# A Flamingo gated layer on one core: the output projection by a 26-product scheme in place of seven products

## The chip, the cores and the metric

The kernel runs on one core of one Trainium2 chip. The metric is the device time of one execution in microseconds (us), here the median of three runs. A profile is one execution recorded by the hardware profiler, with a duration of its own. PE is TensorE's matmul, PEld its weight load, DVE VectorE, ACT ScalarE, POOL GpSimd, SP SyncE (it issues most DMAs).

## The reference

All arrays are fp32. x and ctx are 64 x 128 x 512 (sequences, tokens, DIM). The parts that matter:

```python
xn = layernorm(x)
Q, K, V = heads(xn) @ Wh, heads(ctx) @ Wh, heads(ctx) @ Wh       # 4 heads of 128
A = maximum(abs((Q K^T / sqrt(128) * decay).sum(over the batch)), 1)
Y = groupnorm_like(A @ V) * gamma + beta                         # over DIM
W = relu(xn @ wg)                                                # 512 x 512
x = x + tanh(g_xattn) * ((W * Y) @ wo)                           # wo: 512 x 512
h = silu(ln(x) @ gate_w.T * gate_s) * (ln(x) @ up_w.T * up_s)    # 512 -> 1408
x = x + tanh(g_ffn) * ((h @ down_w.T) * down_s)                  # 1408 -> 512
```

The change is in `(W * Y) @ wo` and its weights alone.

## The kernel before

**Groups.** The 64 sequences are worked on in 16 groups of four (512 tokens, four token tiles of 128). Pass 1 (to about 400 us) normalises every group, sums the scores over the batch, and prepares the weights: `prepare_weights` loads each weight, scales it, forms the sums that the fast schemes need, and writes weights and sums to scratch in DRAM (stores at L481). For wo that is `load_wo` and `sum_wo`: one DVE scale, four POOL sums (L324), seven stores of 256 KB to `wo_scr`.

**Pass 2.** For every group g, `attended(g)` does the output projection, the residual add into the tiles x_t, and the second layer norm; `ffn(g)` does the gated feed-forward part. Ahead of that, `next_retention(g)` makes the gate products W (L287, with adds at L578 and L581 in group 0's neighbourhood), A @ V (`po`, L652/L654), the normalised Y, and W * Y, in the tiles w_t (L711). The generators are interleaved at their yields: in regular groups `ffn(g)` runs beside `attended(g+1)` and then `next_retention(g+2)`. Group 0's projection has only the end of pass 1's work beside it: `in_order("ATATATAAAAAPAPAPAPA", A=attended(0, ...), T=tail, P=...)`. The yields set the order of the text; a list scheduler in the framework then fixes each engine's order of instructions before the launch, and `tc.issue_after` adds constraints to it. Each engine then runs its own list in that order, and waits at semaphores.

**The output projection before.** The 512 x 512 by 512 x 512 product of one group is a 2 x 2 block product by a scheme of seven half-size products. `combine_a` forms four sums (`ys`, 128x512 each) of the four input blocks on `helper`, which is VectorE for groups 0 to 2 and POOL later (L327 to L330). `wo_product` (L725 to L737) loads one weight tile of 256 KB (`wo_w`, L727, tag "wo", three buffers, on SP) and issues four matmuls of 128x128 by 128x256 (L730) into a PSUM bank: bx, bz, bx, by, bz, by, by. After each product the whole bank, 128x512, is added into x_t on DVE (L741); the first is copied by ACT to m1 (L751) and added three times by POOL (L741). A yield stands after each product, and x_t's tiles come from DRAM by `load_x` (L186, pool of five).

**The feed-forward part.** Gate and up use the same seven-product scheme (`product`, L287, banks a, b, c, f), with DVE at L965, L880 and L912 to L918 and ACT at L879; the block that seven products leave over is at L890 to L918 ("rest"), its weights `gu_rest`. The gate/up weights are the tiles `gu` (L849, SP). The down projection already uses the 26-product scheme: `DOWN_STEPS` is a list of 24 steps; a step names an accumulator (c1, a, f, b0, c0, b1), the products that it adds up (indices of a sum of the input, and of a sum of the weights) and the blocks of the output that receive it, with their signs. `H_SUMS` are 28 sums or differences of 128x128 input blocks (L335, `sum_tiles`), `W_SUMS` 18 of 128x256 weight blocks. The down products are L1006, their adds into x_t L1026 (128x256). `last_down` is the last down product issued; the next projection's first product is held behind it.

**PSUM.** Of the eight banks of 128x512 fp32, five belong to the feed-forward part and three (`ps_mm`, tag "mm") rotate among the projection's bx, by, bz and others.

Of the kernel before, what the change touches and what calls it, by code (L numbers as in the profile page):

```python
# [10 lines left out]
F32 = mybir.dt.float32  # L11
AF = mybir.ActivationFunctionType
ALU = mybir.AluOpType
# [10 lines left out]


GA11, GS1, GA12, GS2, GS3, GS4, GA22 = range(7)
DB11, DB21, DB22, DT1, DT2, DT3, DT4 = range(7)

# [7 lines left out]
DOWN_SIGN = (-1, -1, 1, 1, -1, 1, 1, 1)  # L36
H_SLOTS, H_SLOTS3, H_EARLY = 26, 20, 8
H_SUMS = (
# [6 lines left out]
)  # L45
# [6 lines left out]
W_SUMS = (  # L52
# [4 lines left out]
)  # L57
# [13 lines left out]
DOWN_STEPS = (  # L71
    ("c1", ((2, 2, 1),), ((5, -1),)),
    ("a", ((0, 0, 13),), ((0, -1),)),
    ("f", ((8, 8, 10),), ((1, 1),)),
    ("b0", ((20, 1, 12),), ((4, 1), (6, -1),)),
    ("c0", ((6, 6, 2),), ((4, 1),)),
    ("c1", ((22, 13, 15),), ((7, 1),)),
    ("a", ((1, 16, 23),), ((1, -1),)),
    ("f", ((25, 19, 19),), ((0, 1),)),
# [47 lines left out]
def flamingo_gated_layer(  # L127
# [21 lines left out]
    nc = tc.nc  # L149
    P = 128  # L150
    B, S, DIM = x.shape
    H = wh.shape[0]
    INTER = gateT.shape[1]
    NC = DIM // P
    NI = INTER // P
    GB = 4
    NG = B // GB
    TOK = GB * S
    HT = TOK // 2
    HN = DIM // 2  # L160
    KC = NC // 2
# [7 lines left out]
    dram = ctx.enter_context(tc.tile_pool(name="dram", bufs=1, space=DRAM))  # L169
    xin = ctx.enter_context(tc.tile_pool(name="xin", bufs=5))  # L170
    att = ctx.enter_context(tc.tile_pool(name="att", bufs=1))
    wide = ctx.enter_context(tc.tile_pool(name="wide", bufs=2))
    stat = ctx.enter_context(tc.tile_pool(name="stat", bufs=4))
    ps_mm = ctx.enter_context(tc.tile_pool(name="ps_mm", bufs=3, space=PSUM))
    ps_bank = ctx.enter_context(tc.tile_pool(name="ps_bank", bufs=1, space=PSUM))

    last_load, last_norm, last_down, mid_down = [None], [None], [None], [None]
# [40 lines left out]

    gu_scr = [dram.tile([NJ, P, n, 2, KC, P], F32, name=f"gu_scr{n}") for n in (3, 4)]
    dn_scr = dram.tile([26, P, 3, HN], F32, name="dn_scr")  # L220
    wo_scr = dram.tile([7, P, KC, HN], F32, name="wo_scr")
    sq_scr = [
        [dram.tile([P, NQ, NC, GB * SQ], F32, name=f"sq_scr{n}{i}") for i in range(2)]
        for n in range(2)
# [11 lines left out]
    for seeded in (bank_b, bank_c0, bank_c1):  # L236
        for i in range(TOK // P):
            nc.tensor.matmul(
                seeded[:, i * P : (i + 1) * P], lhsT=ident, rhs=ident,
                start=(i == 0), stop=True, skip_group_check=True,  # L240
# [79 lines left out]
    def combine_b(engine, t, b11, b12, b21, b22):  # L320
        for dst, in0, in1 in (
            (t[0], b12, b11), (t[1], b22, t[0]), (t[2], b22, b12), (t[3], b21, t[1]),
        ):
            engine.tensor_tensor(dst, in0, in1, ALU.subtract)  # L324

    def combine_a(engine, s, a11, a12, a21, a22):
        engine.tensor_tensor(s[0], a21, a22, ALU.add)  # L327
        engine.tensor_tensor(s[1], s[0], a11, ALU.subtract)
        engine.tensor_tensor(s[2], a11, a21, ALU.subtract)
        engine.tensor_tensor(s[3], a12, s[1], ALU.subtract)  # L330

    def sum_tiles(engine, slots, sums):

        for to, a, b, sign in sums:
            engine.tensor_tensor(  # L335
                slots[to], slots[a], slots[b], ALU.add if sign == "+" else ALU.subtract
            )
# [4 lines left out]
    once = pass1.enter_context(tc.tile_pool(name="once", bufs=1))  # L342
# [4 lines left out]
    for m, k, e in ((GA11, 0, 0), (GA12, 1, 0), (7, 0, 1), (GA22, 1, 1)):  # L347
        for s in range(2):
            e0 = e * HN + s * P
            nc.sync.dma_start(  # L350
                out=wgc[:, m, s],
                in_=wg[k * HN : (k + 1) * HN, e0 : e0 + P].rearrange("(k p) i -> p k i", p=P),
# [9 lines left out]
    tanh_g = const.tile([P, 2], F32, name="tanh_g")  # L362
# [5 lines left out]
    for h in range(H):  # L368
        nc.tensor.matmul(
            pg[:, h, :], lhsT=whT_sb[:, h, :], rhs=whT_sb[:, h, :],  # L370
            start=True, stop=True,
# [29 lines left out]
    RAW = [P, 8, 2, KC, P]  # L401

    def load_wo():
        raw = once.tile([P, NC, DIM], F32, tag="raw", name="wo_raw", bufs=2)
        nc.sync.dma_start(out=raw, in_=wo.rearrange("(c p) e -> p c e", p=P))
        return raw

    def sum_wo(raw):

        nc.vector.tensor_scalar_mul(ds, ds, tanh_g[:, 1:2])  # L410
        nc.vector.tensor_scalar_mul(raw, raw, tanh_g[:, 0:1])
        t = once.tile([P, 4, KC, HN], F32, tag="sums", name="wo_t")
        b = (
            raw[:, 0:KC, 0:HN], raw[:, 0:KC, HN:DIM], raw[:, KC:NC, 0:HN], raw[:, KC:NC, HN:DIM],
        )
        combine_b(nc.gpsimd, [t[:, i] for i in range(4)], *b)
        return [
            (wo_scr[m], src)
            for m, src in zip(range(7), (b[0], b[2], b[3], t[:, 0], t[:, 1], t[:, 2], t[:, 3]))
        ]  # L420

    def load_down(n):
        raw = once.tile([P, 16, HN], F32, tag="raw", name="dn_raw", bufs=2)
# [168 lines left out]
    for g in range(NG):  # L592
        x_t, c_t = x_next.pop(0), c_next
# [122 lines left out]
    def attended(g, x_t, ws, x1nT):  # L716

        helper = nc.vector if g < 3 else nc.gpsimd

        a11, a21, a12, a22 = ws[0][:, 0], ws[1][:, 0], ws[0][:, 1], ws[1][:, 1]  # L720
        s = att.tile([P, 4, KC, HT], F32, tag="sq", name="ys")
        combine_a(helper, [s[:, i] for i in range(4)], a11, a12, a21, a22)
        yield

        def wo_product(bank, m, lhs, start):  # L725
            w = att.tile([P, KC, HN], F32, tag="wo", name="wo_w", bufs=3)
            nc.sync.dma_start(out=w, in_=wo_scr[m])  # L727
            for i in range(2):
                for k in range(KC):
                    nc.tensor.matmul(  # L730
                        bank[:, i * HN : (i + 1) * HN],
                        lhsT=lhs[:, k, i * P : (i + 1) * P],
                        rhs=w[:, k, :],
                        start=(start and i == 0 and k == 0),
                        stop=(i == 1 and k == KC - 1),
                        skip_group_check=True,
                    )  # L737

        def add(engine, q, cols, src):
            dst = x_t[q][:, :, cols]  # L740
            engine.tensor_tensor(dst, dst, src.rearrange("p (b d) -> p b d", b=2), ALU.add)  # L741

        d1, d2 = slice(0, HN), slice(HN, DIM)
        bx = ps_mm.tile([P, TOK], F32, tag="mm", name="bx")
        if last_down[0] is None:
            wo_product(bx, DB11, a11, True)
        else:
            with tc.issue_after(last_down[0].ins):
                wo_product(bx, DB11, a11, True)
        m1 = att.tile([P, TOK], F32, tag="m1", name="m1")  # L750
        nc.scalar.copy(m1, bx)  # L751
        for q, d in ((0, d2), (1, d2), (1, d1)):
            add(nc.gpsimd, q, d, m1)
        yield
        bz = ps_mm.tile([P, TOK], F32, tag="mm", name="bz")
        wo_product(bz, DT1, s[:, 0], True)
        add(nc.vector, 1, d2, bz)
        yield
        wo_product(bx, DB21, a12, False)
        add(nc.vector, 0, d1, bx)  # L760
        yield
        by = ps_mm.tile([P, TOK], F32, tag="mm", name="by")
        wo_product(by, DT2, s[:, 1], True)
        add(nc.vector, 0, d2, by)
        yield
        wo_product(bz, DB22, s[:, 3], False)
        add(nc.vector, 0, d2, bz)
        yield
        wo_product(by, DT3, s[:, 2], False)
        add(nc.vector, 1, d2, by)  # L770
        yield
        wo_product(by, DT4, a22, False)
        add(nc.vector, 1, d1, by)
        yield

        if g:
            sq = att.tile([P, NQ, NC, GB, SQ], F32, tag="sq", name="sq")
        for j in range(GB):
            xb = x_t[j // 2][:, j % 2, :]
            mv = stat.tile([P, 2], F32, tag="mv", name="mv")  # L780
            bn(mv, xb)
            rs = stat.tile([P, 1], F32, tag="rs", name="rs")
            inv_std(rs, mv[:, 1:2], LN_EPS, 1)
            x1n = normalised(xb, mv[:, 0:1], rs)
            if g:
                square_transposed(sq, j, x1n)
            else:
                pt = transposed(x1n, "pt")
                nc.scalar.copy(
                    x1nT[:, :, :, j, :].rearrange("p i c b -> p c i b"),  # L790
                    pt.rearrange("p c (i b) -> p c i b", i=NQ),
                )
            yield
        if g:
            moved(x1nT, sq, sq_scr[1][g % 2])
# [8 lines left out]
    ws = None  # L804
# [10 lines left out]
    x_t = x_next.pop(0)  # L815
# [242 lines left out]
    for g in range(NG - 1):  # L1058
        x_t = x_next.pop(0)
# [75 lines left out]
```

## Time and profile before

| | |
|---|---|
| median of three runs | 2254.69 us (2254.12 to 2256.78) |
| profiled execution | 2253.64 us, of which the span is 2251.8 us |
| granted clock, mean | 0.998 |
| DMA traffic | 558.46 MB, 248 GB/s |
| wo_w loads | 112 of 256 KB, median 3.6 us from issue to landing |
| period of a regular group | 114.13 us (starts of the first bank_a product: 1193.83, 1307.96, 1422.08) |

The span runs from the first to the last instruction; the rest of the profiled execution's time, 1.84 us, lies around it. Times in views are us from the span's start. Busy TensorE time is a sum of modelled durations; the distance between starts of consecutive matmuls is the surer measure of what one costs.

### The profile page before, as it was taken

The numbers are of one execution on the slowest core, as the hardware profiler recorded it, in microseconds if no ns is written. First come the engines' busy times: TensorE is split into PE (matmuls) and PEld (weight loads), VectorE is DVE, ScalarE is ACT, GpSimd is POOL, SyncE is SP. The second block draws the span as 40 slices with busy tenths as digits, with TensorE's granted clock in tenths as the row PEclk, the third lists the DMA queues.
The fourth block names the chain that finished last, engine by engine and source line by source line (L and its number), as shares of the span: only waits on it lengthen the run. The fifth ranks groups of instructions, "written<-read, shape, count | busy, mean of one in ns | idle before, by whom it ended". The sixth has DMA issues, their size and how long they took to land.

```text
span 2251.8 us, 28752 instructions
## 1 busy us (share of the span) xinstructions
PE 2218.9 (99%) x10112; PEld 1889.7 (84%) x10112; DVE 1190.2 (53%) x2863; ACT 603.3 (27%) x1132; POOL 654.0 (29%) x1038
## 2 busy tenths in 40 slices
PE   8999999999999999999999999999999999999999
PEld 7878787778888888888888888888888888888888
DVE  6456543646454646464646464646464646454524
ACT  3444445322222222222222222222221212121221
POOL 4125300240323333333333333323232324141220
PEclk9999999999999999999999999999999999999999
DMA  9788855678777777777777777777777777766654
GB/s 300 263 279 308 287 190 176 253 240 260 255 269 240 265 249 256 258 248 266 247 267 236 257 247 266 239 262 243 268 237 269 236 272 233 280 205 243 223 184 145
DMA packets 216863, 558.46 MB, mean 248 GB/s; under 512 B 21264, under 2 KB 62992, under 8 KB 199952
## 3 DMA queue, kind: packets, MB, share of 16 engines
q1 hardware_dynamic: 211296, 539.58, 70.9%
q10 hardware_dynamic: 5424, 17.04, 2.0%
q8 instruction: 81, 1.33, 0.2%
q14 instruction: 62, 0.51, 0.1%
HBM read 454.31 MB, written 102.24 MB: 247 GB/s over the span
## 4 chain that ended last, share of the span: by engine, by line
PE 84%; DVE 6%; DMA 5%; POOL 3%; issue 1%; SPq 1%; ACT 0%; ACTq 0%; DVEq 0%; POOLq 0%
PE bank_c L287 18%; PE bank_a L287 12%; PE bank_c L1006 9%; PE bank_b L1006 6%; PE bank_f L287 6%; PE bank_b L287 6%; PE bank_f L1006 4%; PE bank_a L1006 4%; PE by L730 3%; PE sv L538 3%; PE bx L730 3%; PE bz L730 2%; PE po L652 2%; DMA gu_scr<-gu_raw 2%; DVE st L251 2%; PE bank_c L890 2%
## 5 line engine op out<-in xcount | busy, mean ns | idle before, releaser
L287 PE MATMUL bank_c<-tcomb,gu 128*128 128x256 f32 x1920 | 454.9, 380 | 0.7 <-DVE c L965 0.7
L287 PEld LDWEIGHTS bank_c<-tcomb,gu 128*128 128x128 f32 x1920 | 363.3, 190 | 59.3 <-issue 6.7
L335 POOL TENSOR_TENSOR h<-h 128x128 f32<-128x128 f32 x576 | 253.2, 470 | 398.5 <-DVE h L880 282.1
L287 PE MATMUL bank_a<-x1nT,gu 128*128 128x256 f32 x1280 | 305.5, 381 | 11.2 <-DVE h L880 9.6
L287 PEld LDWEIGHTS bank_a<-x1nT,gu 128*128 128x128 f32 x1280 | 241.8, 190 | 62.2 <-DVE h L880 14.8
L1006 PE MATMUL bank_c<-dn_w,h 128*128 128x256 f32 x896 | 211.7, 379 | 0.0
L1006 PEld LDWEIGHTS bank_c<-dn_w,h 128*128 128x128 f32 x896 | 170.2, 190 | 23.2
L879 ACT ACTIVATE sil<-c,gs_sb 128x256 f32<-128x256 f32 x176 | 89.3, 508 | 336.4 <-DVE c L965 171.7
L965 DVE TENSOR_TENSOR c<-bank_c,m 128x512 f32<-128x512 f32 x80 | 55.3, 691 | 219.5 <-PE bank_c L287 219.5
L247 POOL TENSOR_TENSOR rs<-ve,mhalf 128x1 f32<-128x1 f32 x128 | 73.4, 585 | 322.7 <-DVE ve L246 209.8
L711 POOL TENSOR_TENSOR w_t<-w_t,yT 128x256 f32<-128x256 f32 x112 | 91.6, 847 | 258.0 <-ACT yT L702 258.0
L741 POOL TENSOR_TENSOR x_t<-x_t,m 128x512 f32<-128x512 f32 x48 | 62.1, 1323 | 341.4 <-ACT m L751 341.4
L1006 PE MATMUL bank_b<-dn_w,h 128*128 128x256 f32 x640 | 156.4, 379 | 0.0
L335 DVE TENSOR_TENSOR h<-h 128x128 f32<-128x128 f32 x608 | 152.8, 312 | 4.3
L287 PE MATMUL bank_f<-tcomb,gu 128*128 128x256 f32 x640 | 151.2, 379 | 0.0
L287 PE MATMUL bank_b<-x1nT,gu 128*128 128x256 f32 x640 | 151.2, 379 | 0.0
L287 PEld LDWEIGHTS bank_b<-x1nT,gu 128*128 128x128 f32 x640 | 121.6, 190 | 22.1 <-issue 6.2
L287 PEld LDWEIGHTS bank_f<-tcomb,gu 128*128 128x128 f32 x640 | 121.6, 190 | 17.0 <-issue 0.5
L1006 PEld LDWEIGHTS bank_b<-dn_w,h 128*128 128x128 f32 x640 | 121.6, 190 | 16.5
L251 DVE BATCH_NORM_STATS2 st<-x_t 128x6 f32<-128x512 f32 x128 | 83.7, 682 | 79.3 <-DMA x_t<-in_x_dram 78.2
L538 PE MATMUL sv<-qw,c_t 128*128 128x256 f32 x512 | 122.0, 383 | 3.3 <-DVE xnT L513 3.3
L1026 DVE TENSOR_TENSOR x_t<-x_t,bank_c 128x256 f32<-128x256 f32 x192 | 77.8, 420 | 86.9 <-PE bank_c L1006 86.8
(150 smaller groups left out, 3260.8 us busy)
## 6 DMA issues: line engine op xcount, KB each, us to landing
dn_w<-dn_scr SPq DMA_DIRECT2D x320, 384.0 KB, 4.9
gu<-gu_scr SPq DMA_DIRECT2D x80, 1024.0 KB, 7.8
gu<-gu_scr SPq DMA_DIRECT2D x80, 768.0 KB, 5.9
x_t<-in_x_dram SPq DMA_DIRECT2D x62, 512.0 KB, 5.3
sq_scr<-sq SPq DMA_DIRECT2D x30, 1024.0 KB, 4.8
wo_w<-wo_scr SPq DMA_DIRECT2D x112, 256.0 KB, 3.6
dn_w<-dn_scr SPq DMA_DIRECT2D x96, 256.0 KB, 5.2
c_t<-in_ctxT_dram SPq DMA_DIRECT2D x64, 256.0 KB, 4.9
```

The lines of the kernel that those rows point to most:

```text
L247: nc.gpsimd.tensor_tensor(dst, ve, mhalf[:, :n], ALU.pow)
L251: nc.vector.bn_stats(st, src)
L287: nc.tensor.matmul(out, lhsT=w[:, s, k, :], rhs=x_k, start=(start and s == 0 and k == 0), stop=(s == 1 and k == KC - 1), skip_group_check= ...
L335: engine.tensor_tensor(slots[to], slots[a], slots[b], ALU.add if sign == "+" else ALU.subtract)
L538: nc.tensor.matmul(sv[:, 0 : 2 + i : 1 + i, :], lhsT=c_t[j][:, h, :], rhs=qw[:, h, j : GB + 1 : GB - j, :], start=(i == 0), stop=(i == 1), ...
L711: (helper if d else nc.gpsimd).tensor_tensor(w, w, yT[:, :, d * KC + k, q * 2 : q * 2 + 2, :], ALU.mult)
L730: nc.tensor.matmul(bank[:, i * HN : (i + 1) * HN], lhsT=lhs[:, k, i * P : (i + 1) * P], rhs=w[:, k, :], start=(start and i == 0 and k == 0 ...
L741: engine.tensor_tensor(dst, dst, src.rearrange("p (b d) -> p b d", b=2), ALU.add)
L879: nc.scalar.activation(sil, gate, AF.Silu, scale=gs_sb[:, i : i + 1])
L965: nc.vector.tensor_add(c22, bank_c, m5)
L1006: last_down[0] = nc.tensor.matmul(places[acc], lhsT=hq[q][:, a, :], rhs=dn[n][:, q, :], start=start, stop=True, skip_group_check=True,)
L1026: add = nc.vector.tensor_tensor(dst, dst, places[acc], ALU.add if sign > 0 else ALU.subtract)
```

## The change

The output projection takes over the 26-product scheme of the down projection: four token tiles, four tiles of DIM as the inner dimension, and two halves of the output. A group now has 26 single matmuls of 128x128 by 128x256, in the order of `DOWN_STEPS` (first indices). The 28 `H_SUMS` are formed on `helper`, partly in place in the w_t tiles, partly in ten tiles `more` (tag "sq", name ys). The six accumulators lie in halves of the three banks: c1 and b0 in bx, a and c0 in by, f and b1 in bz. After each step one to two DVE adds or subtractions of 128x256 go into x_t, 28 in all; ACT's copy m1 and POOL's adds are gone. A weight tile of 256 KB serves two products: 13 loads, three buffers as before. A yield stands after every fourth product. In the preparation `sum_wo` scales eight blocks by 128x256 with their signs on DVE, forms 18 sums on POOL and makes 26 stores of 128 KB. In the changed kernel the matmul is L751, the weight load L745, the x_t add L762, the down products L995 and their adds L1015.

```diff
-    wo_scr = dram.tile([7, P, KC, HN], F32, name="wo_scr")
+    wo_scr = dram.tile([13, P, 2, HN], F32, name="wo_scr")
...
     def load_wo():
-        raw = once.tile([P, NC, DIM], F32, tag="raw", name="wo_raw", bufs=2)
-        nc.sync.dma_start(out=raw, in_=wo.rearrange("(c p) e -> p c e", p=P))
+        raw = once.tile([P, 16, HN], F32, tag="raw", name="wo_raw", bufs=2)
+        nc.sync.dma_start(
+            out=raw[:, 0 : 2 * NC].rearrange("p (c d) e -> p c d e", d=2),
+            in_=wo.rearrange("(c p) (d e) -> p c d e", p=P, d=2),
+        )
         return raw
...
-        nc.vector.tensor_scalar_mul(raw, raw, tanh_g[:, 0:1])
-        t = once.tile([P, 4, KC, HN], F32, tag="sums", name="wo_t")
...
-        combine_b(nc.gpsimd, [t[:, i] for i in range(4)], *b)
...
+        for i, sign in enumerate(DOWN_SIGN):
+            nc.vector.tensor_scalar(
+                raw[:, i], raw[:, i], tanh_g[:, 0:1], float(sign), ALU.mult, ALU.mult
+            )
+        more = once.tile([P, 10, HN], F32, tag="sums", name="wo_t")
+        slots = [raw[:, i] for i in range(16)] + [more[:, i] for i in range(10)]
+        sum_tiles(nc.gpsimd, slots, W_SUMS)
+        order = [w for _, products, _ in DOWN_STEPS for _, _, w in products]
+        return [(wo_scr[n // 2, :, n % 2], slots[w]) for n, w in enumerate(order)]
...
-        a11, a21, a12, a22 = ws[0][:, 0], ws[1][:, 0], ws[0][:, 1], ws[1][:, 1]
-        s = att.tile([P, 4, KC, HT], F32, tag="sq", name="ys")
-        combine_a(helper, [s[:, i] for i in range(4)], a11, a12, a21, a22)
+        more = att.tile([P, H_SLOTS - 16, P], F32, tag="sq", name="ys")
+        slots = [
+            ws[b // 2][:, k // KC, k % KC, b % 2 * P : (b % 2 + 1) * P]
+            for k in range(NC) for b in range(GB)
+        ]
+        slots += [more[:, i] for i in range(H_SLOTS - 16)]
+        sum_tiles(helper, slots, H_SUMS)
         yield
-        def wo_product(bank, m, lhs, start):
...
-        def add(engine, q, cols, src):
...
+        banks = [ps_mm.tile([P, TOK], F32, tag="mm", name=name) for name in ("bx", "by", "bz")]
+        left, right = slice(0, HN), slice(HN, TOK)
+        places = {
+            "c1": (0, left), "a": (1, left), "f": (2, left),
+            "b0": (0, right), "c0": (1, right), "b1": (2, right),
+        }
+        begun = [None, None, None]
+        after = last_down[0]
+        n = 0
+        for acc, products, to in DOWN_STEPS:
+            bank, cols = places[acc]
+            sums = banks[bank][:, cols]
+            for a, _, _ in products:
+                if n % 2 == 0:
+                    w = att.tile([P, 2, HN], F32, tag="wo", name="wo_w", bufs=3)
+                    nc.sync.dma_start(out=w, in_=wo_scr[n // 2])
+                with ExitStack() as order:
+                    if after is not None:
+                        order.enter_context(tc.issue_after(after.ins))
+                    if begun[bank] is not None:
+                        order.enter_context(tc.issue_after(begun[bank].ins))
+                    first = nc.tensor.matmul(
+                        sums, lhsT=slots[a], rhs=w[:, n % 2],
+                        start=begun[bank] is None, stop=True, skip_group_check=True,
+                    )
+                begun[bank] = begun[bank] or first
+                n += 1
+                if n % 4 == 0:
+                    yield
+            for block, sign in to:
+                b, d = block // 2, block % 2
+                dst = x_t[b // 2][:, b % 2, d * HN : (d + 1) * HN]
+                nc.vector.tensor_tensor(dst, dst, sums, ALU.add if sign > 0 else ALU.subtract)
         yield
```

More of the change, by code (lines that the diff above doesn't have):

```diff
@@ L26 @@
 GA11, GS1, GA12, GS2, GS3, GS4, GA22 = range(7)
-DB11, DB21, DB22, DT1, DT2, DT3, DT4 = range(7)
 DOWN_QUADS = ((0, 1, 6, 5), (2, 3, 8, 7), (10, 9, 4))
@@ L410, in sum_wo @@
         nc.vector.tensor_scalar_mul(ds, ds, tanh_g[:, 1:2])
-        nc.vector.tensor_scalar_mul(raw, raw, tanh_g[:, 0:1])
-        t = once.tile([P, 4, KC, HN], F32, tag="sums", name="wo_t")
-        b = (
-            raw[:, 0:KC, 0:HN], raw[:, 0:KC, HN:DIM], raw[:, KC:NC, 0:HN], raw[:, KC:NC, HN:DIM],
-        )
-        combine_b(nc.gpsimd, [t[:, i] for i in range(4)], *b)
[L417 to L420, printed above, removed]
+        for i, sign in enumerate(DOWN_SIGN):
[7 more added lines that the diff above has]
+        return [(wo_scr[n // 2, :, n % 2], slots[w]) for n, w in enumerate(order)]
     def load_down(n):
@@ L718, in attended @@
         helper = nc.vector if g < 3 else nc.gpsimd
-        a11, a21, a12, a22 = ws[0][:, 0], ws[1][:, 0], ws[0][:, 1], ws[1][:, 1]
-        s = att.tile([P, 4, KC, HT], F32, tag="sq", name="ys")
-        combine_a(helper, [s[:, i] for i in range(4)], a11, a12, a21, a22)
-        yield
-        def wo_product(bank, m, lhs, start):
[L726 to L736, printed above, removed]
-                    )
@@ L739, in add @@
-        def add(engine, q, cols, src):
[L740 to L773, printed above, removed]
+        more = att.tile([P, H_SLOTS - 16, P], F32, tag="sq", name="ys")
[3 more added lines that the diff above has]
+        ]
```

## Prediction

> **What bounds the kernel now.** I read the page first.
>
> ```profile
> PE 2218.9 (99%) x10112; PEld 1889.7 (84%) x10112; DVE 1190.2 (53%) x2863; ACT 603.3 (27%) x1132; POOL 654.0 (29%) x1038
> ...
> PE 84%; DVE 6%; DMA 5%; POOL 3%; issue 1%; SPq 1%; ACT 0%; ACTq 0%; DVEq 0%; POOLq 0%
> ...
> wo_w<-wo_scr SPq DMA_DIRECT2D x112, 256.0 KB, 3.6
> ```
>
> TensorE is busy 99% and carries 84% of the chain that ends last, so a matmul less is time won, if nothing new makes TensorE wait. Second, the waits of PE in the regular groups (560 to 2100 us):
>
> ```profile
> PE bank_a L287 <- DVE h L880: 9.6, 13, 0.9
> ```
>
> That is the only wait, 0.74 us per group. Third, the windows; the columns are length, busy time of PE and PEld, DVE, ACT, POOL, clock, DMA share:
>
> ```profile
> 400.00:440.00 40.00, 36.73 (x164) 27.33 (x163) 27.14 (x60) 15.60 (x28) 10.79 (x13) 1.00 0.63 242
> 440.00:480.00 40.00, 37.48 (x165) 32.02 (x164) 19.48 (x43) 12.96 (x24) 17.10 (x34) 0.96 0.57 192
> 1112.00:1226.00 114.00, 113.27 (x517) 97.62 (x516) 61.24 (x152) 26.38 (x50) 35.35 (x60) 1.00 0.76 255
> ```
>
> A regular group leaves TensorE nothing idle; the first two groups (first two rows) leave it 3.3 and 2.5 us, so there other engines already end last. Fourth, the groups by line, with shapes apart (minimum/median/maximum in ns):
>
> ```profile
> L730 PE MATMUL bx<-wo_w,w_t x256: 379/379/631, 412.2 to 2057.4; 128*128 128x256 f32 x128
> L741 POOL TENSOR_TENSOR x_t<-x_t,m x48: 1262/1271/1462, 419.8 to 2051.5; 128x512 f32<-128x512 f32 x48
> L741 DVE TENSOR_TENSOR x_t<-x_t,by x48: 651/686/689, 424.6 to 2075.1; 128x512 f32<-128x512 f32 x48
> L1026 DVE TENSOR_TENSOR x_t<-x_t,bank_c x192: 412/421/423, 531.2 to 2246.6; 128x256 f32<-128x256 f32 x192
> L335 DVE TENSOR_TENSOR h<-h x608: 277/286/1355, 449.5 to 2221.8; 128x128 f32<-128x128 f32 x152
> L335 POOL TENSOR_TENSOR h<-h x576: 443/455/899, 450.5 to 2198.5; 128x128 f32<-128x128 f32 x192
> ```
>
> L730 is the seven-product projection; L1026 and L335 are the same kinds of add and sum that the change brings in, so they price it. The profile records two matmuls for one of the program (896 at L730 for 28 in each of 16 groups). Eight records start every 1.727 us (1141.16, 1142.88, 1144.61), so one program matmul costs 0.432 us of TensorE, though its modelled duration is 379 ns.
>
> **Matmuls removed.** 26 stand in place of 28: −2 × 0.432 = −0.863 us in each of 16 groups, −13.8 us in all. That is the whole gain.
>
> **Work beside TensorE, regular groups.** VectorE: 28 adds of 128x256 by 0.421 are 11.8 us against six by 0.686, 4.1 us; with 61.2 of 114 us busy that is no bound. GpSimd: 28 sums of 128x128 by 0.455 to 0.470 are 13 us against four sums of 1.27 and three adds of 1.27, 8.9 us. Today the sums end at 1112.5 and the first product starts at 1133.4; the new ones end some 8 us later, about 1121, and stay covered; without that cover they would cost up to 8 us a group. The ScalarE copy (0.59 us) goes. Loads: 13 tiles of 256 KB instead of 7, 1.5 MB more a group beside 558 MB in all: no bandwidth question, but each tile lands for two matmuls (0.86 us) instead of four (1.73), with three buffers as before, and a load on SyncE's queue now waits for TensorE 13 times with the gate/up loads behind it. I cost that at nothing, since no wait of PE for a gu tile shows today; if that slack is gone, the price is up to one landing (7.8 us for 1 MB by the page) a group.
>
> **New waits in a regular group.** The instruction order of the changed kernel spreads the products between the same feed-forward matmuls as before, and every product waits for the last add that read its bank, either half: six accumulators take turns in three banks. One turn, from rows: the add starts 0.20 us after the next PE group, lasts 0.42, and PE follows 0.06 later (1193.77 to 1193.83): 0.68 us, or 1.6 matmuls. With two adds it is about 1.0 us, 2.35 matmuls. Placed on the matmul pitch from 1128.2 on, all turns just fit, and these are the thin ones. The add that comes first now needs the x_t half, loaded at 1129.75 and landed at 1134.35 (4.6 us); today the first reader is GpSimd, later:
>
> ```profile
> 1128.41 0.42 DVE L1026 TENSOR_TENSOR x_t<-x_t,bank_b 128x256 f32<-128x256 f32 x1 [1.74 <-PE bank_b L1006]
> ...
> 1136.25 0.42 DVE L912 TENSOR_TENSOR c<-bank_c,m 128x256 f32<-128x256 f32 x1 [7.42 <-PE bank_c L890]
> ...
> 1138.73 1.55 DVE L335 TENSOR_TENSOR h<-h 128x128 f32<-128x128 f32 x2
> 1141.41 0.69 DVE L741 TENSOR_TENSOR x_t<-x_t,bz 128x512 f32<-128x512 f32 x1 [1.13 <-issue]
> ```
>
> So that add runs 1134.42 to 1134.85, and the next product of its bank stands at 1135.12: slack 0.2 us, gone if the load takes the page's median for x_t, 5.3 us; behind the add in VectorE's queue stand L912 and L915, for which the L890 matmuls wait. The other thin turns have 0.05 to 0.6 us. One tile is needed at 1144.2 and lands at 1143 to 1145 (landing 2.5 to 5.2 us): 0 to 0.8 us. I take 0.4 for the tile and 0.2 for the rest, 0.6 us a group (ends 0.15, if only one slack fails, and 1.5, if the tile and x_t fail by 0.7 each): −0.863 + 0.6 = −0.26, in the 14 groups from 2 on −3.7 us (−10 to +8.9). Below nothing the stalls could go only by the 0.74 us wait for L880: two L335 sums took 1.55 us while GpSimd added m, and those three adds are gone from there; I give it no value, since L880 itself is not faster.
>
> The Trainium skill, page "PSUM — Partial Sum Buffer", section "PSUM bank collisions raise a hardware error", says that PSUM must be guarded by bank and quadrant, not by address: two engines in disjoint columns of one bank collide. It speaks against counting six accumulators as six; no run here shows a collision. If halves were free, only x_t and the tile would be left of the thin waits, and this term would be some 2 us better.
>
> **Group 0.** Its sums run on VectorE, between the adds that the gate product next to them waits for:
>
> ```profile
> 414.58 0.69 DVE L329 TENSOR_TENSOR ys<-w_t 128x512 f32<-128x512 f32 x1 [1.88 <-POOL w_t L692]
> ...
> 416.52 0.68 DVE L578 TENSOR_TENSOR w<-bank_c,m5p 128x512 f32<-128x512 f32 x1
> ...
> 422.36 0.69 DVE L741 TENSOR_TENSOR x_t<-x_t,bz 128x512 f32<-128x512 f32 x1 [3.23 <-POOL x_t L741]
> ...
> 431.01 0.69 DVE L741 TENSOR_TENSOR x_t<-x_t,by 128x512 f32<-128x512 f32 x1
> ```
>
> In the new order the 28 sums, 28 × 0.25 to 0.31 = 7.0 to 8.7 us where four took 2.75, stand ahead of the L578 add; PE's next gate product and all behind it start about 4.3 us later, at 421.8 instead of 417.5. Then little feed-forward work lies between the products, and three tile buffers set the pace: a tile lands in 2.5 to 2.9 us there, is used for 0.86 and released, (2.75 + 0.86 + 0.1) / 3 = 1.24 us a tile, 13 tiles 16.1 us against 13 × 0.86 = 11.2 of matmul. The last add then ends near 421.8 + 16.1 + 1.5 = 439.4 instead of 431.7. The layer norm, and by it FFN(0), wait for it: +7.7, taken as +8. Ends: +4 (the sums alone) and +12 (the page's 3.6 us landing: 1.52 us a tile, 19.8 us). The page "DMA: Bandwidth & Descriptors", in its fixed-cost fit, gives 2.0 us plus bytes / 436e3, an estimate of 2.6 us a tile, which would make this term about 0.7 us smaller; the rows here go from 2.5 to 3.6.
>
> **Groups 1 and 2, pass 1.** Group 1's sums are VectorE's too, 28 × 0.286 − 4 × 0.69 = 5.3 us more, where TensorE already waits 2.5 us for the projection's input; I put 3 us on the path, the rest in the 4.9 us that VectorE waits there for GpSimd, less the 0.86 saved: +2.2 (0 to 6). Group 2's lie in the down phase, covered. Preparation: 18 sums of 128x256 by 0.85 against four of 1.4, 10 us more on GpSimd, idle 17.8 us at that place; 26 stores instead of 7 on SyncE (about 15 against 8 us at 65 to 74 us) ahead of x_t and gu_raw loads: +1 (0 to 4), or 0 if the raw loads have the slack.
>
> **Sum.** −3.7 + 8 + 2.2 + 1 = +7.5 us on the profiled 2253.64 us (span 2251.8 and 1.84 around it): 2261.1. The median is 1.05 us above the profiled run, so 2262.2.
>
> **Rivals.** *The waits fit.* Steady stalls 0.15 us, group 0 only +4, groups 1 and the preparation free: 14 × −0.71 + 4 = −6 us, 2248.7. For it: every wait has positive slack on paper, and TensorE is the bound. Against: group 0, where the order puts the sums first. It decides if group 0's loss stays under 5 us, from which on the result is faster or even. *The turns do not fit.* Stalls of 1.5 us a group turn the steady part to +8.9: 8.9 + 8 + 2.2 + 1 = +20, 2274.8. For it: landing times spread by more than the slacks. Against: slack lost once is partly regained by the next turn. *Even.* Steady stalls 0.6 and group 0 at +4, the first groups otherwise free: +0.3 to +3, about 2256.
>
> **Numbers.** A measurement of this kernel tells about 0.2%, 4.5 us. Forecast (first two groups lose more than the rest gains) 0.40, fitting waits 0.27, turns that do not fit 0.17, even 0.16. Faster 0.27, same 0.16, slower 0.57. Range 2246 to 2277: from steady gains of −0.8 a group with a cheap start to the third case with 2 us more.
>
> **What would show it.** Right: regular period near 113.9 us (114.13 now), with waits of products (now L751) for the x_t adds (L762), x_t or wo_w; 7 to 9 us lost between 411 and 440; wait at the gate product for the L578 add. Wrong: the first FFN starts within 3 us of today's time; a period of 113.3 (waits fit) or above 114.7 (turns fail); waits behind gu loads, which I cost at nothing.

## The result and the profile after

The changed kernel takes 2325.73 us (median of 5, 2322.05 to 2333.41) where the one before takes 2254.69: 1.0316 times as long, 95% interval 1.0296 to 1.0337. The forecast was 2262.2 us, at most 2277. The sign was right; the loss was 71 us where 7.5 were forecast.

First rows from the page of the profile after: the share of each engine, the chain that ended last, and two rows of DMA loads.

```profile
PE 2232.9 (96%) x10048; PEld 1878.4 (81%) x10048; DVE 1335.6 (57%) x3294; ACT 592.3 (25%) x1116; POOL 702.1 (30%) x1316
...
PE 71%; DMA 14%; DVE 11%; POOL 2%; SPq 1%; issue 1%; ACT 0%; DVEq 0%; POOLq 0%; ACTq 0%
...
wo_w<-wo_scr SPq DMA_DIRECT2D x208, 256.0 KB, 3.7
x_t<-in_x_dram SPq DMA_DIRECT2D x62, 512.0 KB, 6.4
```

TensorE has 64 records fewer (two per group, each recorded twice), and its share of the chain fell from 84% to 71%; DMA took 14% of it where it had 5%, VectorE 11% where it had 6%. The work went away; waits came in its place. The waits of PE from 560 to 2160 us (engine, line and releaser; total, times, longest):

```profile
PE bx L751 <- DVE x_t L762: 19.0, 14, 2.9
PE bx L751 <- DMA wo_w<-wo_scr: 10.6, 12, 2.0
PE bank_a L287 <- DVE h L869: 9.4, 13, 0.7
PE bank_f L995 <- DVE x_t L1015: 4.2, 10, 0.4
PE bank_b L995 <- DVE x_t L1015: 4.0, 12, 1.5
```

Of these only the third was there before. And one regular group and the stretch of group 0 in the windows (the third column from the end is the granted clock, the share of its full speed that TensorE had):

```profile
1057.90:1175.10 117.20, 113.80 (x513) 96.64 (x512) 70.58 (x174) 25.67 (x49) 39.54 (x80) 1.00 0.77 260
...
425.00:465.00 40.00, 29.61 (x100) 19.75 (x99) 25.00 (x72) 5.59 (x10) 2.51 (x4) 0.83 0.76 274
```

The ledger, from the starts of the same products in both traces; FFN(g) stands for the first matmul of group g's feed-forward part. The 481st of the 512 records of score products, near the end of pass 1, is 8.3 us later (392.8 against 384.5); the first product of the projection 11.6 (423.84 against 412.21); from it to the last product's end 27.0 us against 18.8, +8.2; from there to FFN(0) 11.0 against 2.4, +8.6. FFN(0) to FFN(1) is +1.25. Thirteen regular periods are 117.16 us against 114.15, +39.2, and the last one is +3.1. The sum, 11.6 + 8.2 + 8.6 + 1.25 + 39.2 + 3.1 = 72 us, is the difference of the spans (2323.9 and 2251.8). In the prediction's terms: regular groups −3.7 forecast, +42.3 measured; group 0 +8 and +20.1 (3.3 of it between the end of pass 1 and the first product); group 1 +2.2 and +1.25; pass 1 +1 and +8.3. The regular groups failed most.

Why did the first add of a regular group wait? VectorE's timeline of one down phase and the start of the next group (start, length, engine, line, tiles, idle before and releaser):

```profile
1041.28 6.13 DVE L324 TENSOR_TENSOR tcomb<-x1nT 128x512 f32<-128x512 f32 x2
1047.34 0.41 DVE L1015 TENSOR_TENSOR x_t<-x_t,bank_f 128x256 f32<-128x256 f32 x1
...
1058.10 0.42 DVE L1015 TENSOR_TENSOR x_t<-x_t,bank_b 128x256 f32<-128x256 f32 x1 [1.74 <-PE bank_b L995]
1066.26 0.42 DVE L762 TENSOR_TENSOR x_t<-x_t,bx 128x256 f32<-128x256 f32 x1 [7.74 <-DMA x_t<-in_x_dram]
```

Two things are to be seen. The first x_t add waits 7.74 us for the load of x_t, which was issued at 1059.66 and landed at 1066.14, 6.5 us where the prediction carried over 4.6; TensorE, which began the first product at 1063.1, stands still before the next product of that bank until 1066.83. Why this load landed later is not shown; the median of the x_t loads rose from 5.3 to 6.4 us. And two tcomb subtractions (VectorE's sums for the gate and up products of the next group) took 6.13 us while GpSimd went through its sums:

```profile
1041.02 1.27 POOL L335 TENSOR_TENSOR w_t<-w_t 128x128 f32<-128x128 f32 x3
1042.26 0.86 POOL L335 TENSOR_TENSOR ys<-w_t,ys 128x128 f32<-128x128 f32 x2
```

In the kernel before, the same pair took 1.29 us, and began when GpSimd's four sums had just ended (1112.5):

```profile
1112.77 1.29 DVE L324 TENSOR_TENSOR tcomb<-x1nT 128x512 f32<-128x512 f32 x2
```

In group 0 the ledger has a cause that no wait shows: three stretches in which TensorE ran at half its clock, where the kernel before had 1.00 from 411 to 440 us.

```profile
429.70:433.10 3.40, 3.40 (x10) 2.65 (x9) 2.28 (x6) 1.06 (x1) 0.00 (x0) 0.50 0.17 42
440.00:443.40 3.40, 3.40 (x10) 2.27 (x8) 1.24 (x3) 0.00 (x0) 0.00 (x0) 0.50 0.46 146
453.60:460.40 6.80, 5.76 (x15) 3.49 (x16) 3.59 (x10) 1.52 (x3) 2.37 (x4) 0.50 1.01 399
```

TensorE was busy for 12.6 us in them; half of that, about 6 us, is an estimate of what the lower clock cost: 3.4 us among the products and 2.9 after them.

### The profile page after: what moved, and what is told of

Same layout as the page of the kernel before. It is cut to its first block, busy times and chain, and to the rows that moved or that the text cites. A ratio compares the mean times of both kernels' runs of the same rounds, so it can differ in the third digit from the quotient of the medians.

```text
span 2323.9 us, 29598 instructions
## 1 busy us (share of the span) xinstructions
PE 2232.9 (96%) x10048; PEld 1878.4 (81%) x10048; DVE 1335.6 (57%) x3294; ACT 592.3 (25%) x1116; POOL 702.1 (30%) x1316
## 4 chain that ended last, share of the span: by engine, by line
PE 71%; DMA 14%; DVE 11%; POOL 2%; SPq 1%; issue 1%; ACT 0%; DVEq 0%; POOLq 0%; ACTq 0%
PE bank_c L287 17%; PE bank_a L287 10%; PE bank_c L995 7%; PE bank_b L287 6%; PE bank_f L287 6%; DMA x_t<-in_x_dram 5%; DMA wo_w<-wo_scr 4%; PE sv L540 4%; PE bank_b L995 4%; DVE tcomb L324 3%; PE bank_a L995 3%; PE bx L751 2%; PE bank_f L995 2%; PE by L751 2%; PE po L654 2%; PE bz L751 2%
## 5 line engine op out<-in xcount | busy, mean ns | idle before, releaser
L287 PE MATMUL bank_c<-tcomb,gu 128*128 128x256 f32 x1920 | 465.3, 380 | 0.7 <-ACT bank_b L943 0.7
L995 PE MATMUL bank_c<-dn_w,h 128*128 128x256 f32 x896 | 211.7, 379 | 0.0
L995 PEld LDWEIGHTS bank_c<-dn_w,h 128*128 128x128 f32 x896 | 170.2, 190 | 23.2
L762 DVE TENSOR_TENSOR x_t<-x_t,bx 128x256 f32<-128x256 f32 x160 | 64.0, 416 | 175.8 <-DMA x_t<-in_x_dram 89.4
L995 PE MATMUL bank_b<-dn_w,h 128*128 128x256 f32 x640 | 157.7, 381 | 4.0 <-DVE x_t L1015 4.0
L995 PEld LDWEIGHTS bank_b<-dn_w,h 128*128 128x128 f32 x640 | 120.6, 190 | 24.8 <-DVE x_t L1015 8.9
L335 DVE TENSOR_TENSOR h<-h 128x128 f32<-128x128 f32 x608 | 137.8, 284 | 4.4
L1015 DVE TENSOR_TENSOR x_t<-x_t,bank_c 128x256 f32<-128x256 f32 x192 | 76.7, 417 | 77.7 <-PE bank_c L995 77.6
```

The source lines that it names most:

```text
L287: nc.tensor.matmul(out, lhsT=w[:, s, k, :], rhs=x_k, start=(start and s == 0 and k == 0), stop=(s == 1 and k == KC - 1), skip_group_check= ...
L335: engine.tensor_tensor(slots[to], slots[a], slots[b], ALU.add if sign == "+" else ALU.subtract)
L762: nc.vector.tensor_tensor(dst, dst, sums, ALU.add if sign > 0 else ALU.subtract)
L995: last_down[0] = nc.tensor.matmul(places[acc], lhsT=hq[q][:, a, :], rhs=dn[n][:, q, :], start=start, stop=True, skip_group_check=True,)
L1015: add = nc.vector.tensor_tensor(dst, dst, places[acc], ALU.add if sign > 0 else ALU.subtract)
```

## The experiments

The theory after this view: a regular group loses four waits to three causes (x_t loaded just in time; tiles with three buffers; GpSimd's sums against tcomb), and the six accumulators in three banks are no cause. The rival: the turns of the banks cost by themselves, so that a wait taken away comes back at the next product. Ratios are to the kernel before, in the same set of runs; the changed kernel stands at 1.0316. A gain that an expectation names is against the kernel that it starts from.

**Six x_t buffers.** With five buffers, the second tile of a group's pair is loaded only when the out store of the group two before has freed it.

```diff
-    xin = ctx.enter_context(tc.tile_pool(name="xin", bufs=5))
+    xin = ctx.enter_context(tc.tile_pool(name="xin", bufs=6))
```

> The changed kernel (2325.7 us) with six x_t buffers in place of five, so that the second half of a group's x_t is loaded a group earlier and no longer waits for an out store (room made by halving the tile of zeros; the ACT copy of bank_b becomes two). Theory (the first add waits for the x_t landing, and the next product of bank bx for that add, 1.3 to 2.9 us in 14 groups, 19.0 us): the wait goes, 15 to 25 us faster, about 2306 us. Rival (the turns of the three banks do not fit anyway): the wait goes to another product, under 5 us change.

Measured 2314.2 us, 1.0268 (1.0251 to 1.0286). The wait for L762 is gone from the regular groups and their period fell from 117.16 to 115.69 us, about 20 us in all, as the theory had it; but the whole gained only 11 us, less than expected, for pass 1 became 7.6 us longer (last score products 15.9 us late instead of 8.3). The spare buffer did that too: with it added only after pass 1, below, they were 6.6 us late.

**Sums behind tcomb.** (For groups 3 to 15; `tok_last` holds the tile tcomb made last.)

```diff
...
+            end = tok_last[0][:, 3, 0, 0, 0:1]
+            pin = nc.gpsimd.tensor_tensor(seen, end, end, ALU.add)
+            with tc.issue_after(pin.ins):
+                sum_tiles(helper, slots, H_SUMS)
...
```

> The changed kernel with GpSimd's 28 input sums of groups 3 to 15 held behind the last tcomb subtraction by a GpSimd add of 128x1 that reads it. Theory (GpSimd's sums and VectorE's two-input tcomb subtractions exclude each other: two of them took 6.13 us, 1.29 us in the kernel before; behind them the down products wait 0.6 us a group and the out stores, and so the x_t loads, are later): tcomb back to about 1.3 us a pair, no L995 waits (8.2 us), 8 to 16 us faster. Rival (that cost is hidden; later sums make the first products wait): between no change and 20 us slower.

Measured 2305.66 us, 1.0225 (1.0207 to 1.0244), 20 us where 8 to 16 were expected; period 115.71. The waits for L1015 (8.2 us) are gone, and those for x_t adds fell from 19.0 to 14.4 us, those for tiles from 10.6 to 8.0. The groups of tcomb by line, shapes apart (minimum/median/maximum ns), first of the changed kernel, then of this one:

```profile
L324 DVE TENSOR_TENSOR tcomb<-x1nT x26: 731/941/5294, 687.0 to 2098.7; 128x512 f32<-128x512 f32 x26
```

```profile
L325 DVE TENSOR_TENSOR tcomb<-x1nT x26: 682/684/685, 685.9 to 2074.8; 128x512 f32<-128x512 f32 x26
```

One subtraction took up to 5.3 us beside GpSimd's sums and never more than 0.69 without them, while the adds with an operand in PSUM stayed at 0.41 to 0.42. The Trainium skill, page "SBUF — State Buffer", section "SBUF: two separate sides", has the rule for it: a VectorE operation with two SBUF inputs and a GpSimd operation that reads SBUF lock each other out for the whole instruction. The trace agrees, and shows more: VectorE's subtraction began at 1041.28 and ended at 1046.55, while GpSimd went through eleven sums back to back, 0.45 us each.

**Four wo_w buffers.** (`bufs=3` to `bufs=4` for the tag "wo".)

> The changed kernel with four wo_w buffers in place of three. Theory (tiles land too late since a load waits for TensorE to free one of three buffers, 10.6 us of waits in the regular groups, 3.5 us in group 0): 6 to 12 us faster. Rival (the landing is late by what is queued ahead on the DMA engines, or the wait is hidden behind the x_t wait): under 3 us change.

Measured 2293.09 us, 1.0173 (1.0157 to 1.019): 32 us where 6 to 12 were expected. The period fell by 1.56 us to 115.60. The waits for tiles went, and of those for x_t adds 19.0 fell to 10.4 us; that a late tile shifts what follows it would explain this, but is argued, not shown. Group 1 gained 6.5 us and group 0 about 3.

**All three.**

> The changed kernel with the three edits at once: six x_t buffers, the sums behind tcomb, four wo_w buffers (room made by moving two small tiles that pass 1 alone uses). Theory (three waits of about 1 us each are all that a regular group lost; the bank turns fit): only the wait for L869/L880 is left, the period is 113.3 us or a little less (114.13 before, 117.2 in the changed kernel), 2262 to 2272 us in all, what remains over 2254.7 being pass 1 and group 0. Rival (the turn-taking of the three banks is itself a cost of a regular group): waits of products for x_t adds stay, period 114.1 or more, 2278 us or more.

Measured 2267.37 us, 1.007 (1.0054 to 1.0087). The waits of PE in its regular groups:

```profile
PE bank_a L288 <- DVE h L878: 9.4, 13, 0.7
PE bank_c L288 <- ACT bank_b L952: 0.7, 1, 0.7
```

That is the whole list. No product of the projection waits any more, and the period is 113.27 us: 114.15 less 0.88, against 0.863 reckoned for two matmuls. So the rival falls: turn-taking in three banks cost a regular group nothing that can be seen, and the gain of the scheme is real once its waits are gone.

**Pass 1: where the stores stand.** Two edits of the changed kernel against the same 8.3 us: the 26 stores from ScalarE's queue, or only two stores.

> The changed kernel with the 26 wo stores of pass 1 issued from ScalarE's queue in place of SyncE's. Theory (26 stores ahead of the x_t and ctx loads on SyncE's queue make pass 1 late by 6.4 us at 100 to 114 us): 5 to 8 us faster. Rival (the bytes, not the queue, or ScalarE is held up by the stores in its place): under 2 us, or slower.

Measured 2322.51 us, 1.0301 (1.0281 to 1.0322), not to be told from the changed kernel. The score products were 9.2 us late at the end of pass 1, and 9.0 already at the 49th record, where the changed kernel was only 2.7 late: the delay moved to the engine that now carried the stores. ScalarE's own work stood behind them four times from 40 to 110 us, for 4.8, 3.9, 3.4 and 2.2 us.

```diff
-        return [(wo_scr[n // 2, :, n % 2], slots[w]) for n, w in enumerate(order)]
+        return [
+            (wo_scr[0:16].rearrange("m p e -> p m e"), raw),
+            (wo_scr[16:26].rearrange("m p e -> p m e"), more),
+        ]
```

> The changed kernel with one edit: wo's 26 blocks written by two stores, and loaded two at a time by a strided slice. Theory (the 26 issues on SyncE's queue delay the x_t loads behind them; with six x_t buffers another delay hid this): the score products of pass 1 are late by 2 to 3 us instead of 8.3 at the 128th, 4 to 8 us faster, about 2319 us. Rival (18 sums on GpSimd ahead of its rstd, or the bytes, make pass 1 late): under 2 us.

Measured 2319.12 us, 1.0296 (1.0264 to 1.0328). By time alone that is no more than the noise, but the trace has the step by itself: the score products end pass 1 1.1 us late in place of 8.3. VectorE's waits for x_t at 90 to 120 us say how the stores had made them late; in turn the changed kernel, the kernel before, and the one with two stores:

```profile
DVE st L251 <- DMA x_t<-in_x_dram: 14.8, 3, 9.1
```

```profile
DVE st L251 <- DMA x_t<-in_x_dram: 8.7, 2, 6.2
```

```profile
DVE st L251 <- DMA x_t<-in_x_dram: 13.2, 3, 6.8
```

The sum stays high, but the longest wait, 9.1 us, is gone. An x_t load issued at 89.43 us before, and at 98.91 in the changed kernel, is issued at 88.54 with two stores.

Now the three edits with the sixth x_t buffer added after pass 1 alone (the ring), and then with two stores as well:

> The three edits together (2267.4 us), with the sixth x_t buffer added only after pass 1. Theory (with six buffers in pass 1 the score products were late by 15 us instead of 8.3, since the x_t loads take another place on SyncE's queue): 6 to 9 us faster, about 2260 us, the regular period still 113.3 us. Rival (the order after pass 1 shifts and the x_t or tile waits return): period above 113.6, or no gain.

> As the run before, with the two stores. Theory: another 4 to 8 us out of pass 1, about 2254 us, even with the kernel before. Rival (pass 1 is late by the sums, or loads of 1 KB rows land later and stall group 0): no gain.

Measured 2260.12 us (1.0028, 1.0017 to 1.0039) and 2256.7 us (1.0012, 1.0001 to 1.0023), both with a period of 113.27. The first gained 7 us, as expected; the second 3.4 more, a little less than the 4 to 8 expected, and the trace has 3.6 of it in pass 1. The second is the best version found. It lies within the 0.2% that can be told here, with an interval just above 1: not faster than the kernel before.

**Group 0.** In the best version FFN(0) still starts 21.6 us later than before (455.05 against 433.41); group 1 gives back 6.0 and the thirteen regular periods 11.4. What holds group 0 was looked for in more runs. First the order of the token tiles, in all groups and in group 0 alone; "the run before" is the version with all three edits (2267.37 us) for the first, and the best version (2256.7 us) for the second:

> As the run before, with the four token tiles of the scheme assigned to the sequences in another order, (3, 0, 2, 1), so that sequences 0 and 1, which FFN(0) reads first, get their last add at steps 19 and 21 of 24 and not at the last. Theory (in group 0 FFN(0) began 10.6 us after the last add, 1.7 us in the kernel before, since sequence 0 is finished by the very last product and the layer norm follows it): 3 to 8 us faster than without. Rival (the last add and the queue behind it set the start, whichever sequence it is for): under 1.5 us.

> As the run before, with the token tiles reordered in group 0 alone, (3, 0, 2, 1), so that sequences 0 and 1 end early there and the regular groups keep their order. Theory (of the 10 us from the last add to FFN(0) some 3 go, as in the run that permuted all groups, without its waits for L878 in the regular groups): 2 to 4 us faster, about 2251 us. Rival (the last product comes later by as much, as it did there by 2.4 us): within 1.5 us.

The first took 2290.89 us (1.0167, 1.0152 to 1.0182), 23.5 us more than without where 3 to 8 less were expected: FFN(0) began 6.3 us after the last product in place of 9.7, but the regular groups waited twice as often for L878 (25.5 us, 27 times) and their period rose to 114.71. The second took 2263.74 us (1.0033, 1.0014 to 1.0053), slower too: FFN(0) began 5.3 us earlier than without, and FFN(1) 5.7 us later. Two more runs went on from the version permuted in all groups. Two stores there gave 2291.67 us, no gain where 6 to 8 us were expected; with group 0's sums on GpSimd as well it was 2297.46 us, 5.8 us slower, as its rival had it:

> As the run before, with wo's 26 blocks written by two stores in place of 26 (blocks in their own order; a load takes two blocks by a strided slice, one block once). Theory (the 26 issues on SyncE's queue, about 0.5 us each, put the x_t loads of pass 1 at 86.2 and 98.9 us in place of 79.4 and 89.4): pass 1 gets back 6 to 8 us. Rival (18 sums on GpSimd make it late, or the 1 KB rows make the later loads slower): under 2 us, or slower.

> As the run before, with group 0's 28 sums on GpSimd in place of VectorE. Theory (on VectorE they stand ahead of the gate add, L580, for which the gate product and the products behind it wait 2.0 us): 2 to 4 us faster. Rival (GpSimd takes 0.46 us a sum where VectorE takes 0.2 to 0.28, so the products wait for sums instead): 2 to 6 us slower.

From the best version again: group 0's tiles, its sums, and the place of its sums:

> The version with ring and two stores (2256.7 us), with group 0's weight blocks loaded whole, ahead, into two tiles that pass 1 no longer needs, so that no product of group 0 waits for a tile. Theory (in group 0 the tile loads set the pace of the products, as the prediction had it: 1.24 us a tile): the stretch from the first product to the last, 25.3 us, falls by 3 to 6 us, about 2252 us. Rival (the turns of the banks with the adds, or the late gate add, set the pace): under 1.5 us.

> The same version with group 0's 28 sums left out (its products take unsummed blocks, so group 0's output is not the reference's). Theory (the sums on VectorE hold up the gate add and the products behind it): 3 to 6 us faster, which is their price. Rival (tiles, turns and the layer norm set the end of group 0, and the sums lie beside them): under 1.5 us.

> The same version with the last three gate steps written ahead of group 0's projection (TTTAAA in place of ATATAT), so that the gate adds stand ahead of the sums on VectorE. Theory (TensorE's waits of 2.0 us for the gate add go): 1 to 3 us faster. Rival (the sums and with them the products start later by as much, and no gate product is left to lie between the products): same or up to 4 us slower.

Measured 2262.8 us (1.004, 1.0027 to 1.0053), 2261.16 us (1.0031, 1.0021 to 1.0041) and 2266.67 us (1.0055, 1.0037 to 1.0072). All three are slower than the version without (1.0012). In the stretch that they were made for, the first two theories held: from the first product to the last 21.0 and 21.2 us where it was 25.3. In the third the wait for the gate add went and the stretch was 20.8 us, but two gate products, 3.5 us of matmuls, now stand ahead of it, and its first product came 2.5 us later: its rival held. Yet from FFN(0) to FFN(1) each took 127 to 129 us where the version without took 118. The waits of PE from 470 to 620 us with the tiles loaded ahead, the two longest:

```profile
PE bank_a L1025 <- DMA dn_w<-dn_scr: 3.8, 1, 3.8
PE bank_c L289 <- DVE c L983: 2.7, 1, 2.7
```

The whole stretch from FFN(0) to FFN(1) in the windows, first of the best version, then with the tiles loaded ahead:

```profile
455.05:573.00 117.95, 114.51 (x514) 96.11 (x513) 88.91 (x262) 30.03 (x56) 28.05 (x56) 1.00 0.81 271
```

```profile
447.12:575.98 128.86, 118.90 (x514) 99.18 (x513) 90.50 (x262) 30.31 (x56) 27.88 (x56) 0.96 0.74 249
```

The matmuls are the same. TensorE is idle 10.0 us in place of 3.4, and its work takes 4.4 us longer at a granted clock of 0.96. To see whether VectorE's sums in group 1 hold it, these were given to GpSimd (without the hold behind tcomb that the later groups have), without and with the tiles loaded ahead:

> The version with ring and two stores (2256.7 us), with the sums of groups 1 and 2 on GpSimd as in the groups after, in place of VectorE. Theory (in group 1 VectorE's sums stand ahead of the adds that FFN(0) waits for): group 1, 118.0 us from FFN(0) to FFN(1), falls by 1 to 4 us, about 2254 us, even with the kernel before or a little better. Rival (GpSimd's sums come too late for group 1's first products): 1 to 4 us slower.

> As the run before, with group 0's weight blocks also loaded whole, ahead. Theory (group 0's products get through 4.3 us earlier, as measured, and with VectorE free in group 1 the gain is not lost there again to the wait for its adds, 2.7 us, and for a down tile, 3.8 us): about 2250 us, 0.1 to 0.3% faster than the kernel before. Rival (group 1 is paced by the SyncE queue, which holds the down tiles behind the transposing transfers of the next group, whatever VectorE does): FFN(1) starts no earlier than without the tiles, 2256 us or more.

Measured 2265.61 us (1.0048, 1.0031 to 1.0065) and 2261.03 us (1.0033, 1.0022 to 1.0044). The two waits went, and products now waited 3.8 and 1.6 us for GpSimd's sums; with the tiles ahead FFN(1) began no earlier (575.8 us against 576.0), without them later (582.5 against 573.0). Both are slower than the best version; for the second that is what its rival said. So group 1 is not ready for an earlier group 0, on whichever engine its sums stand. In all six versions that lost there (the order of group 0 alone, tiles, sums, place, and these two) TensorE is idle 8.7 to 10.7 us between FFN(0) and FFN(1) and runs at a clock of 0.96 to 0.99, where the best version has 3.4 us and 1.00: the time goes to waits and to slower matmuls. What sets these waits, the SyncE queue or the chain from group 1's normalisation to its sums, stays open.

## Why the prediction was wrong, by its steps

**Right.** Two matmuls less are worth 0.863 us a group: 0.88 measured where nothing else intervened. All bank turns fit in the regular groups: no product waited for a turn once x_t, tiles and sums were in time. So the rule that the prediction quotes from the Trainium skill, page "PSUM — Partial Sum Buffer", section "PSUM bank collisions raise a hardware error", to guard by bank and not by address, is kept there at no price.

**Near in size, partly by luck.** Group 0's products stretch from 18.8 to 27.0 us, +8.2, for which the text had +7.7 by late sums and 1.24 us a tile. Both causes are there, and smaller than thought: TensorE waited 2.0 us for the gate add (4.3 in the text) and 3.5 us for tiles (4.9); taking either away from the best version gave 4 us back. What filled the gap is the half-speed clock, about 3.4 us, which the text did not have.

**"Slack 0.2 us, gone if the load takes the page's median."** The wait was seen, and priced at part of 0.2 us. It measured 1.36 us a group (19.0 us in 14), and the edit that removed it 1.47. The mistake was to carry the landing time of one load in the old order, 4.6 us, into an order with six more loads a group, and to hold the median against it as a mere possibility.

**"I take 0.4 for the tile."** Mis-sized: a fourth buffer was worth 1.56 us a group, and 10 us in groups 0 and 1. The text placed each tile by itself. With three buffers a load cannot be issued before TensorE has freed a tile, so a late product delays the next loads as well; that this is how 1.56 came about is argued, not shown. The 2.6 us a tile that the prediction sets beside its rows comes from a fit that the Trainium skill, page "DMA: Bandwidth & Descriptors", section "Anatomy of one DMA — SWDGE (gpsimd) path", gives for transfers issued by GpSimd; these loads are SyncE's, and took 3.7 us (median).

**"The new ones end some 8 us later, about 1121, and stay covered."** This cover was the step that failed outright: the collision stood in the sum at nothing, and it measured 1.45 us a group, with the waits that came of it. The sums did end before their first product, but in those 8 us tcomb stands on VectorE (from 1112.77 in the kernel before), and the two excluded each other. What runs at the same time on the other engine was not asked, only who needs the result. The sign of it stood in the prediction's own text, two VectorE sums that took 1.55 us "while GpSimd added m".

Together 4.5 us a group by single edits, 3.9 in combination (117.16 to 113.27): they overlap a little. With all three edits the thirteen periods gained 11.4 us.

**"+1 (0 to 4)" for pass 1.** It was 8.3, 7.2 of which the two stores gave back. The mechanism was named (stores ahead of x_t on SyncE's queue), the size was not worked out from what waits for those loads: an x_t load issued 9.5 us later (98.91 against 89.43) when TensorE had no slack for it. TensorE then waited 4.5 us in one piece (95 to 120 us).

**Group 0's end.** The text had the layer norm behind the last add, but let it cost what it did before. With seven products sequences 0 and 1 were complete two products of four matmuls before the end; in `DOWN_STEPS` sequence 0 gets its last add from the last product, and statistics, transposes and copies follow it: +8.6 us not in the sum. TensorE waits 3.8 us there for the layer norm, and then loses an estimated 2.9 to the half-speed clock; the rest, about 2 us, is transposes and A @ V products that now stand ahead of FFN(0). Ahead of the first product 3.3 us more were lost: a gate product of four matmuls (1.73 us) now precedes it, and TensorE waits 1.7 us before it for a copy by ScalarE. Group 1, by contrast, cost 1.25 us, not 2.2. The rival in which the turns do not fit came nearest in time, 2274.8 us, and named a wrong cause.

## What to carry to other kernels

Before counting removed work as gain, list for every added instruction the engine beside it, the queue ahead of it and the buffer behind it: here 28 small sums cost nothing where they stood in the schedule and 1.45 us through the engine beside them, and one buffer more of 256 KB, alone, was worth 32 us. A scheme with more, smaller steps needs its operands earlier and in more pieces, so look at what is loaded just in time and buffer it before judging the scheme. And time won at one place counts only if the stage after it was waiting for it: four microseconds won in group 0 never arrived at FFN(1). Look at the granted clock of the stretch as well as at its waits: in group 0 it took about 6 us that no list of waits has.

## What was not expected of the hardware

In group 0 of the best version TensorE waited 3.9 us for the layer norm, and then ran its next matmuls at half speed. Windows of that stretch:

```profile
444.00:448.00 4.00, 0.63 (x3) 0.20 (x2) 3.29 (x10) 0.00 (x0) 0.54 (x1) 0.76 0.84 309
448.00:452.00 4.00, 3.46 (x11) 2.35 (x12) 2.39 (x8) 0.59 (x1) 1.98 (x3) 0.50 0.99 380
452.00:455.00 3.00, 3.00 (x13) 1.66 (x13) 0.79 (x3) 1.66 (x3) 0.00 (x0) 0.84 1.00 348
455.00:459.00 4.00, 3.55 (x17) 2.74 (x16) 3.90 (x8) 1.80 (x4) 0.00 (x0) 1.00 1.03 397
```

The granted clock fell to 0.50 after the wait and came back some 5 us later; by these rows (3.46 us at 0.50 and 3.00 at 0.84) a wait of about 4 us cost about two more, an estimate. Shorter waits did it too. In a regular group of the changed kernel a wait of 2.86 us ended at 831.11, and soon after the clock was at half for 3.4 us:

```profile
831.11 0.67 PE L751 MATMUL bx<-wo_w,ys 128*128 128x256 f32 x2 [2.86 <-DVE x_t L762]
```

```profile
832.50:835.90 3.40, 3.40 (x10) 2.64 (x9) 1.31 (x4) 0.51 (x1) 0.00 (x0) 0.50 0.94 333
```

Of the eleven idle gaps over 1.2 us in these fourteen periods, the two longest (2.86 and 2.50 us) had such a stretch at their end or soon after it, the others (up to 2.24 us) none. But in group 0 of that kernel waits of 1.7 and 2.0 us, 5 us apart, were enough (429.70 above). So no single length decides here. The Trainium skill, page "TensorE: Matmul & The Clock Gate", section "HAM oscillation — how this bites in real kernels", puts the limit at idle gaps of more than about 3.4 us. The wait of 3.9 us agrees with it, those of 2.5 and 2.86 us do not, and the measurement decides.
